# Dividing layer 0's attention probabilities on GpSimd or ScalarE in a kernel whose order is planned, with new strand ranks

## The chip, the cores and the metric

The kernel runs on one core of one Trainium2 chip. The metric is device time in microseconds (us) of one execution, lower is better. The engines are named as in the profile: PE is TensorE's matmul (PEld its weight load), DVE is VectorE, ACT is ScalarE, POOL is GpSimd, SP is SyncE, which only issues DMAs here.

## The reference, cut to what matters

Two transformer layers on 16 x 256 = 4096 tokens of width 128, all in float32; every half layer ends in a residual sum and a layer norm.

```python
# layer 0 attention: 16 heads of 64, over 256 tokens of a batch element
h = rmsnorm(x) * norm_scale
q, k, v = h @ wq, h @ wk, h @ wv               # (16, 256, 16, 64) each
weights = softmax(q * 64**-0.5 @ k^T)          # over 256 keys: the probabilities
x = layernorm(x + (weights @ v) @ w_out + b_out)
# layer 0 feed-forward: 8 routed experts (hidden 256), top 2, and a shared one
x = layernorm(x + shared(x) + sum over top 2 of prob * expert(x))
# layer 1 attention: for each token, 16 heads of 8 attend to each other
scores = q @ k^T / 8                           # (16 x 16) for each token
x = layernorm(x + (softmax(scores) @ v) @ Wproj + bproj)
# layer 1 feed-forward: 8 experts (hidden 512), top 2
x = layernorm(x + sum over top 2 of prob * expert(x))
```

Softmax is exp(s - max) divided by its sum. The change is about who does that division in layer 0's attention, and about the order of everything.

## The kernel before, in words

**Groups, units, parts.** The 4096 tokens are 8 groups of 512 (two batch elements each), held on the chip as tiles `x0` to `x7`. Layer 0's attention works in 128 units: a unit is one pair of heads of one batch element, so a group has 16 units. A unit takes these steps: four score matmuls into a PSUM tile `s` of 128 x 1024 (`scores`, L574); the negated row maximum on DVE (L537); four exponentials on ACT that write `pr` and add up their sums `su` (L543); the reciprocal `rs` on DVE (L554); four multiplications of `pr` by `rs` on POOL (L558, the division); eight transposes of `pr` on PE (`turn`, L591), copied out of PSUM as `pT` (`copied`, L270 on DVE or L272 on ACT); four matmuls with the values into `po` (`attended`, L612), copied out as `oT`. Around these stand the projections `pq`, `pk` (L510) and `pv` (L528) and, once for every half of a group, the output projection `py` (L629, L649). `attention0` walks through the units in order; the transposes and value matmuls of a unit come three units after its scores (`LAG = 3`).

**Waves.** A group whose attention is done goes on as a "part". Parts are joined into waves (`WAVES`): five for layer 0's feed-forward (groups 0, 1, 2+3, 4+5, and 6 with half of 7) and three for layer 1's (0 to 3, 4+5, 6+7). I write (0,4) for layer 0's last wave and (1,2) for layer 1's last. A wave is routed (`chosen`, `route`; L853 writes where each row goes), its rows are scattered to DRAM by expert with indirect DMAs that POOL issues (`send`, L905), read back in blocks of four tiles of 128 rows (`lists`: rows L1014, transposes `px` L1060, first matmuls `ph` L1098, GELU on ACT L1071 or L1077, second matmuls `po_e` L1118, copies `yq`), and gathered again by POOL's indirect DMAs (L934) and added with their gates (L948). Between the layers each part runs through layer 1's attention (`attention1`, `chunk1`), in chunks of 128 tokens. It has no matmuls for scores: products `qk_prod` on DVE (L1216) and their sums (L1220), the maximum, a subtraction on POOL or DVE (L1245), the exponential on ACT (L1254), products `av_prod` with the values in two halves, each on POOL or on DVE (L1292), and sums again on DVE (L1267). After `attention0` is over, a piece of these sums may be done by PE instead (L1226), when the planner finds PE free enough (`SUMS`). The second half of group 7 does not go through the lists: `sequence` and `dense` run all experts over its 256 tokens (`ph_d` L1528, `po_d` L1541).

**The planner.** No scheduler reorders anything. All of the above are Python generators ("strands"). Each yields the time from which its next piece can run and the engine it needs; `everything` (L322) takes again and again the strand with the least start minus `time`, ties by `rank`, and lets it issue one piece. `time` and `rank` are the numbers in `KEYS`; `PACE` gives the rank of the attention units by half group. `work` (L228) advances a clock for each engine by a cost written in the source, for example 2.05 for the four divisions. The order of issue, and so each engine's in-order queue, is fixed when the program is built. The same clocks decide choices between engines: `copied` (L262) takes DVE if its end plus `COPY` is not later than ACT's; `chunk1` takes POOL or DVE for the subtraction and `av_prod` with `FAVOUR` as the margin. `function` (L253) books a change of ACT's function table when exp follows gelu or the other way round; `SWITCH` and `SWITCH_BACK` add to the start of a strand that would need one.

**What the change touches.** `KEYS`, `PACE`, `COPY`, `SUMS`, `FAVOUR`, `SWITCH`, `SWITCH_BACK` (L150 to L194), and `softmax` (L532 to L559), which `scores` starts once for each unit. After the division the unit's time is noted under `end["p", u]`, which `turn` waits for.

Of the kernel before, what the change touches and what calls it, by code (L numbers as in the profile page):

```python
# [10 lines left out]
AF = mybir.ActivationFunctionType  # L11
ALU = mybir.AluOpType
# [25 lines left out]
def two_layers(  # L38
# [23 lines left out]
    nc = tc.nc  # L62
# [75 lines left out]
    def cleared(layer, w):  # L138
# [10 lines left out]

    INF = float("inf")  # L150
    KEYS = {
        "copy qk": (-0.897, 0.036),
        "copy v": (-2, 0.466),
        "copy p": (0.219, 0.818),
        "copy o": (-2, 0.246),
        "softmax": (-0.178, 0.347),
        "softmax 2": (-1.887, 0.235),
        "summed": (-1.203, 0.424),
        "normalised": (-0.822, 0.486),
        "heads": (-0.667, 0.044),  # L160
        "w route": (0.515, 0.015),
        "w send": (0.14, 0.346),
        "w shared": (-0.361, 0.219),
        "w loads": (-0.176, 0.409),
        "w turns 0": (-1.078, 0.086),
        "w turns 1": (1.714, 0.284),
        "w firsts 0": (-1.18, 0.141),
        "w firsts 1": (-0.671, 0.597),
        "w gelu": (-0.639, 0.186),
        "w seconds 0": (-0.71, 0.566),  # L170
        "w seconds 1": (-0.947, -0.095),
        "w stored": (-0.148, -0.464),
        "w gathered 0": (0.897, 0.302),
        "w gathered 1": (1.266, -0.485),
        "w qkv": (2, 0.577),
        "w attention1": (0.922, 0.081),
        "w attention1 2": (0.862, 0.231),
        "w sums": (0.434, 0.099),
        "w normed": (-1.109, 0.178),
        "d loads": (0.367, 1.088),  # L180
        "d route": (-0.611, 0.589),
        "d firsts": (-0.264, -0.008),
        "d gelu": (0.669, 0.244),
        "d seconds": (0.433, -0.444),
        "d added": (0.222, 0.651),
        "d normed": (-0.464, 0.567),
    }
    PACE = [0.305, 1.929, -0.337, -0.416, 1.268, -0.017, 0.106, 1.867]
    PACE += [1.673, 1.567, 1.23, 2, 1.49, 1.385, 1.46, 2]
    now = [0]  # L190
    COPY = -0.089
    SUMS = 9.857
    FAVOUR = 0.474
    SWITCH, SWITCH_BACK = 0.249, 0.734  # L194
    window, unit = [0, 0.0, 1.0], [P]
    clk = {"PE": 0.0, "DVE": 0.0, "ACT": 0.0, "POOL": 0.0, "SP": 0.0}
    table = ["exp"]
    ends = {"t": [0.0] * 2, "m": [0.0] * 2, "s": [0.0] * 2}
    end = {}
# [8 lines left out]
    def paced(at, us, mode):  # L208

        if mode != unit[0]:  # L210
            unit[0] = mode
            us += 0.09
        w = int(at / W)
        if w > window[0]:
            window[2] = 2.0 if w > window[0] + 1 or window[1] < 0.6 * W else 1.0
            window[:2] = w, 0.0
        us *= window[2]
        while at + us > (w + 1) * W:
            part = (w + 1) * W - at
# [42 lines left out]
    def copied(o, i, *after):  # L262
# [50 lines left out]
    def stage(what, w=0, i=0):  # L313

        running[-1].key = key(what, w, i)
# [119 lines left out]
    sc, nm, pr, su, pT, ya = {}, {}, {}, {}, {}, {}  # L435
# [31 lines left out]
    def normalised(g):  # L467
# [10 lines left out]
        yield at, EITHER  # L478
        if max(clk["DVE"], at) + 1.2 + COPY <= max(clk["ACT"], at) + 1.4:
            for c in range(NC):  # L480
# [16 lines left out]
        hT[g] = sb.tile([P, GT], FP, tag="hT", name=f"hT{g}")  # L497
        if max(clk["DVE"], at) + 0.75 + COPY <= max(clk["ACT"], at) + 0.7:
            nc.vector.tensor_scalar(hT[g], t, nscale_s, None, ALU.mult)
# [32 lines left out]
    def softmax(u, place, at):  # L532

        yield at, "DVE"
        nm[u] = sm.tile([P, 4], FP, tag="nm", name=f"nm{u}", bufs=4)
        s = sc[u].rearrange("p j q k -> p (j q) k")
        nc.vector.tensor_reduce(nm[u], s, AX.X, ALU.max, negate=True)  # L537
        at = work("DVE", 1.25, at)
        yield at, "ACT", "exp"
        pr[u] = sb.tile([P, 4, 256], FP, tag="pr", name=f"pr{u}", bufs=LAG + 2)  # L540
        su[u] = sm.tile([P, 4], FP, tag="su", name=f"su{u}", bufs=4)
        for i in range(4):
            nc.scalar.activation(  # L543
                pr[u][:, i, :],
                s[:, i, :],
                AF.Exp,
                bias=nm[u][:, i : i + 1],
                accum_out=su[u][:, i : i + 1],
            )
        at = closed(place, function(2.0, "exp", at))  # L550
        stage("softmax 2")
        yield at, "DVE"
        rs = sm.tile([P, 4], FP, tag="rs", name=f"rs{u}", bufs=4)
        nc.vector.reciprocal(rs, su[u])  # L554
        at = work("DVE", 0.2, at)
        yield at, "POOL"
        for i in range(4):
            nc.gpsimd.tensor_scalar(pr[u][:, i, :], pr[u][:, i, :], rs[:, i : i + 1], 1.0, ALU.mult, ALU.mult)  # L558
        end["p", u] = work("POOL", 2.05, at, one=0.5)  # L559

    def scores(u):

        g, p, b = UNITS[u]
        if g == LAST:
            yield after(("qk", p, b)), "PE", "s"
            q, k = qT[g, p, b], kT[g, p, b]
        else:
            yield after(("q", g, p), ("k", g, p)), "PE", "s"
            q, k = qT[g, p][:, ts(b, 256)], kT[g, p][:, ts(b, 256)]
        sc[u] = ps_s.tile([P, 2, 2, 256], FP, tag="s", name=f"s{u}")  # L570
        for qc in range(2):
            for j in range(2):
                part = slice(j * DH, (j + 1) * DH)
                nc.tensor.matmul(  # L574
                    sc[u][:, j, qc, :],
                    q[part, ts(qc, P)],
                    k[part, :],
                    start=True,
                    stop=True,
                )  # L580
        begin(softmax(u, opened("s"), work("PE", 0.87, mode=-DH)), key("softmax"))
# [84 lines left out]
    def attention0():  # L666
# [3 lines left out]
        for u in range(len(UNITS) + LAG):  # L670
# [4 lines left out]
            if g < NG:  # L675
                now[0] = 2 * g + i // NP
                running[-1].key = (KEYS["heads"][1], PACE[now[0]], 0, 0)
                if i == 3 and g + 1 < NG:
# [522 lines left out]
    def chunk1(w, c, o, qv, kv, at, sums):  # L1201
# [276 lines left out]
    w = DENSE  # L1478
# [185 lines left out]
```

## Time and profile before

| | us |
|---|---|
| runs: lowest, median, highest of three | 1256.01, 1259.93, 1268.71 |
| the profiled execution, its own time | 1225.47 |
| its span from first to last instruction | 1223.8 |
| PE, DVE, ACT, POOL busy in it | 1094.7, 912.3, 730.8, 700.2 |
| last matmul group of layer 0's attention (`py` L649) ends | 852.0 |
| last routing of layer 1, wave (1,2), done (L853) | 1120.8 |

The mean granted TensorE clock of the profiled execution was 0.962 of full speed. Its time is 2.7% under the median of the runs; the page and the trace describe this one execution.

How to read the views quoted below. A row of the page's groups has line, engine, operation, output and input tiles, their shapes and a count, then the total busy time and the mean of one in ns, then the idle time of the engine just before these instructions and what ended it. A row of the windows view is a stretch of time, its length, the busy time of PE, PEld, DVE, ACT and POOL in it with the number of instructions in brackets, the granted clock, the share of DMA time and GB/s. A row of the timeline has start, duration, engine, line and operation. In a waits row one engine's instruction waits for another's; total, number and the longest follow.

### The profile page before, as it was taken

How to read it: one execution, taken by the hardware profiler on the slowest of the kernel's cores; microseconds unless marked ns; L12 is line 12 of the kernel's file. 1: busy time of each engine (PE TensorE's matmuls, PEld its weight loads, DVE VectorE, ACT ScalarE, POOL GpSimd, SP SyncE). 2: the span in 40 equal slices, each digit the busy share in tenths (PEclk: the TensorE clock that was granted, in tenths of full speed). 3: DMA queues.
4: the chain of work that ended last, by engine and by line, in shares of the span. 5: the costliest groups of instructions: out<-in, count | busy, mean ns of one | idle time of the engine just before them, and what ended most of it. 6: DMA issues, size and time to landing. Idle time of an engine off the chain costs nothing.

```text
span 1223.8 us, 22539 instructions
## 1 busy us (share of the span) xinstructions
PE 1094.7 (89%) x7272; PEld 792.6 (65%) x7272; DVE 912.3 (75%) x1810; ACT 730.8 (60%) x2073; POOL 700.2 (57%) x1085
## 2 busy tenths in 40 slices
PE   9999999989999999988999998898667889778893
PEld 5566667666656665576655666675466779678792
DVE  4767786449889789964788888978896879897333
ACT  6556566666667656766566666765554555355442
POOL 4434363635565547732864775577684745567765
PEclk9999999999999999999999999999777999899997
DMA  8900021441000003043100033315627967876871
GB/s 263 276 1 1 1 85 55 143 134 42 3 1 1 2 1 93 29 126 92 29 1 2 16 106 104 94 46 165 192 87 234 280 204 226 258 217 186 250 227 58
DMA packets 187207, 132.45 MB, mean 108 GB/s; under 512 B 12745, under 2 KB 171474, under 8 KB 187090
## 3 DMA queue, kind: packets, MB, share of 16 engines
q1 hardware_dynamic: 179410, 115.27, 32.1%
q0 software_dynamic: 7680, 15.74, 4.2%
q8 instruction: 58, 0.95, 0.3%
q14 instruction: 59, 0.48, 0.1%
HBM read 97.94 MB, written 33.03 MB: 107 GB/s over the span
## 4 chain that ended last, share of the span: by engine, by line
PE 61%; DVE 13%; POOL 11%; ACT 7%; issue 4%; DMA 3%; SPq 1%; ACTq 0%; DVEq 0%; POOLq 0%
PE s L574 10%; PE po L612 9%; PE t L591 8%; POOL rows L905 7%; PE po_e L1118 4%; PE ph L1098 4%; PE pv L528 4%; PE py L629 4%; PE pq L510 4%; PE pk L510 3%; POOL pr L558 2%; DVE av_prod L1292 2%; DVE o L1267 2%; DVE qk_prod L1216 1%; ACT h L1077 1%
## 5 line engine op out<-in xcount | busy, mean ns | idle before, releaser
L558 POOL TENSOR_SCALAR pr<-pr,rs 128x256 f32<-128x256 f32 x512 | 245.8, 497 | 259.6 <-DVE rs L554 172.1
L543 ACT ACTIVATE pr<-s,nm 128x256 f32<-128x256 f32 x512 | 236.0, 476 | 12.3 <-DVE nm L537 9.6
L537 DVE TENSOR_REDUCE nm<-s 128x4 f32<-128x1024 f32 x128 | 156.2, 1220 | 60.2 <-PE s L574 59.6
L1098 PE MATMUL ph<-xqT,wa 128*128 128x128 f32 x1028 | 141.0, 293 | 26.1 <-ACT h L1077 9.0
L905 POOL DMA_INDIRECT rows<-x,r_pi x120 | 131.9, 1099 | 40.9 <-issue 20.6
L1098 PEld LDWEIGHTS ph<-xqT,wa 128*128 128x128 f32 x1028 | 131.9, 204 | 35.1 <-ACT h L1077 11.6
L934 POOL DMA_INDIRECT y<-outs,r_pi x120 | 122.5, 1021 | 52.9 <-issue 23.1
L591 PE MATMUL t<-ident,pr 128*128 128x128 f32 x1024 | 141.8, 279 | 4.9 <-ACT pT L272 1.7
L612 PE MATMUL po<-pT,v 128*64 128x256 f32 x1024 | 141.0, 394 | 2.2 <-DVE kT L270 0.9
L591 PEld LDWEIGHTS t<-ident,pr 128*128 128x128 f32 x1024 | 111.5, 141 | 48.4 <-POOL pr L558 23.0
L270 DVE COPY pT<-t 128x512 f32<-128x512 f32 x171 | 111.7, 686 | 35.4 <-PE t L591 35.0
L574 PEld LDWEIGHTS s<-kT,qT 64*128 64x128 f32 x896 | 77.5, 187 | 82.4 <-issue 65.8
L574 PE MATMUL s<-kT,qT 64*128 64x256 f32 x896 | 127.9, 404 | 0.0
L272 ACT COPY oT<-po 128x256 f32<-128x256 f32 x102 | 38.0, 373 | 137.1 <-PE po L612 136.9
L543 ACT ACTIVATION_READ_ACCUMULATOR pr<-s,nm 128x1 f32 x512 | 105.9, 207 | 0.0
L612 PEld LDWEIGHTS po<-pT,v 128*64 128x64 f32 x1024 | 63.0, 136 | 62.2 <-issue 18.3
L1292 POOL TENSOR_TENSOR av_prod<-sc,qkv 128x1024 f32<-128x1024 f32 x34 | 86.4, 2550 | 28.7 <-ACT sc L1254 28.3
L1216 DVE TENSOR_TENSOR qk_prod<-qkv 128x1024 f32<-128x1024 f32 x64 | 82.9, 1295 | 0.0
L1267 DVE TENSOR_REDUCE o<-av_prod 128x64 f32<-128x1024 f32 x64 | 75.8, 1200 | 8.5 <-POOL av_prod L1292 8.2
L1220 DVE TENSOR_REDUCE sc<-qk_prod 128x128 f32<-128x1024 f32 x64 | 78.1, 1220 | 2.2
L1118 PE MATMUL po_e<-wb,h 128*128 128x128 f32 x648 | 76.3, 276 | 2.1 <-DVE lg L738 1.5
L1118 PEld LDWEIGHTS po_e<-wb,h 128*128 128x128 f32 x648 | 74.4, 192 | 3.6 <-DVE lg L738 1.9
(230 smaller groups left out, 1972.6 us busy)
## 6 DMA issues: line engine op xcount, KB each, us to landing
wa<-in_w_dram SPq DMA_DIRECT2D x190, 128.0 KB
wa<-in_w_dram SPq DMA_DIRECT2D x81, 256.0 KB
wb<-in_w_dram SPq DMA_DIRECT2D x81, 256.0 KB
xq<-rows SPq DMA_DIRECT2D x38, 256.0 KB
outs<-yq SPq DMA_DIRECT2D x38, 256.0 KB
rows<-clear SPq DMA_DIRECT2D x3, 1472.0 KB
rows<-clear SPq DMA_DIRECT2D x1, 2496.0 KB
rows<-clear SPq DMA_DIRECT2D x2, 1216.0 KB
```

What stands on the lines that cost most here:

```text
L270: nc.vector.tensor_copy(o, i)
L537: nc.vector.tensor_reduce(nm[u], s, AX.X, ALU.max, negate=True)
L543: nc.scalar.activation(pr[u][:, i, :], s[:, i, :], AF.Exp, bias=nm[u][:, i : i + 1], accum_out=su[u][:, i : i + 1],)
L558: nc.gpsimd.tensor_scalar(pr[u][:, i, :], pr[u][:, i, :], rs[:, i : i + 1], 1.0, ALU.mult, ALU.mult)
L574: nc.tensor.matmul(sc[u][:, j, qc, :], q[part, ts(qc, P)], k[part, :], start=True, stop=True,)
L591: nc.tensor.transpose(t[:, kc, ts(qc, P)], pr[u][:, 2 * j + qc, ts(kc, P)], ident)
L612: nc.tensor.matmul(po[j * DH : (j + 1) * DH, :], vs[g, p // 4, 2 * b + kc][:, ts(h, DH)], pT[u][j][:, kc, :], start=(kc == 0), stop=(kc == 1),
L905: i = nc.gpsimd.indirect_dma_start(out=rows[layer][w][:, :], out_offset=bass.IndirectOffsetOnAxis(ap=r.pos[:, k, c : c + 1], axis=0), in_= ...
L934: nc.gpsimd.indirect_dma_start(out=y, out_offset=None, in_=outs[layer][w][:, :], in_offset=bass.IndirectOffsetOnAxis(ap=r.pos[:, k, c0 + c ...
L1098: nc.tensor.matmul(ph[:, q - q0, c, :], was[i, q][0][:, c, :], xTs[i][0][:, q, :], start=True, stop=True)
L1118: nc.tensor.matmul(po[:, q, :], hs[i, q][0][:, c, :], wbs[i, q][0][:, c, :], start=(c == 0), stop=(c == nh - 1))
L1292: (nc.gpsimd if e == "POOL" else nc.vector).tensor_tensor(m, sc1[:, ts(j, HALF)].unsqueeze(2).to_broadcast(full), v3.unsqueeze(1).to_broad ...
```

## The change

The division of a unit's probabilities (L558) may now be issued on ACT too: as four activations with the identity function and the reciprocal as scale. The planner takes POOL if the end it sees there is not later than ACT's end plus `FAVOUR`. All ranks and times of the strands, the paces and the margins have new values; `FAVOUR` goes from 0.474 to 1.062, `SUMS` from 9.857 to 4.434. No other function differs. Lines of the changed kernel from L557 on are shifted: the division on POOL is L559 there, on ACT L563, and everything behind it stands five lines lower.

```diff
     KEYS = {
-        "copy qk": (-0.897, 0.036),
-        "copy v": (-2, 0.466),
-        "copy p": (0.219, 0.818),
+        "copy qk": (0.304, 0.033),
+        "copy v": (-0.269, 0.523),
+        "copy p": (0.383, 1.08),
...
-        "softmax": (-0.178, 0.347),
-        "softmax 2": (-1.887, 0.235),
+        "softmax": (-0.066, 0.509),
+        "softmax 2": (-1.427, 0.071),
...
     }
-    PACE = [0.305, 1.929, -0.337, -0.416, 1.268, -0.017, 0.106, 1.867]
-    PACE += [1.673, 1.567, 1.23, 2, 1.49, 1.385, 1.46, 2]
+    PACE = [1.852, -1.516, -1.265, -1.123, 0.732, 0.983, 1.152, 1.417]
+    PACE += [0.679, 0.685, 1.48, 0.579, 0.99, -1.924, -0.939, 1.947]
     now = [0]
-    COPY = -0.089
-    SUMS = 9.857
-    FAVOUR = 0.474
-    SWITCH, SWITCH_BACK = 0.249, 0.734
+    COPY = 0.039
+    SUMS = 4.434
+    FAVOUR = 1.062
+    SWITCH, SWITCH_BACK = 0.202, 0.754
...
         at = work("DVE", 0.2, at)
-        yield at, "POOL"
-        for i in range(4):
-            nc.gpsimd.tensor_scalar(pr[u][:, i, :], pr[u][:, i, :], rs[:, i : i + 1], 1.0, ALU.mult, ALU.mult)
-        end["p", u] = work("POOL", 2.05, at, one=0.5)
+        yield at, ("POOL", "ACT")
+        if max(clk["POOL"], at) + 2.05 <= max(clk["ACT"], at) + 1.55 + FAVOUR:
+            for i in range(4):
+                nc.gpsimd.tensor_scalar(pr[u][:, i, :], pr[u][:, i, :], rs[:, i : i + 1], 1.0, ALU.mult, ALU.mult)
+            end["p", u] = work("POOL", 2.05, at, one=0.5)
+        else:
+            for i in range(4):
+                nc.scalar.activation(pr[u][:, i, :], pr[u][:, i, :], AF.Identity, scale=rs[:, i : i + 1])
+            end["p", u] = work("ACT", 1.8, at)
```

More of the change, by code (lines that the diff above doesn't have):

```diff
@@ L151, in two_layers @@
     KEYS = {
-        "copy qk": (-0.897, 0.036),
-        "copy v": (-2, 0.466),
-        "copy p": (0.219, 0.818),
-        "copy o": (-2, 0.246),
-        "softmax": (-0.178, 0.347),
-        "softmax 2": (-1.887, 0.235),
[L158 to L186, printed above, removed]
-    }
-    PACE = [0.305, 1.929, -0.337, -0.416, 1.268, -0.017, 0.106, 1.867]
-    PACE += [1.673, 1.567, 1.23, 2, 1.49, 1.385, 1.46, 2]
+        "copy qk": (0.304, 0.033),
+        "copy v": (-0.269, 0.523),
@@ new lines, in two_layers @@
+        "copy p": (0.383, 1.08),
+        "copy o": (-1.601, 0.246),
+        "softmax": (-0.066, 0.509),
+        "softmax 2": (-1.427, 0.071),
+        "summed": (-0.419, 0.032),
+        "normalised": (1.073, 0.277),
+        "heads": (-0.14, 0.067),
+        "w route": (0.494, 0.045),
+        "w send": (0.024, 0.635),
+        "w shared": (0.015, 0.221),
+        "w loads": (0.751, 0.707),
+        "w turns 0": (-2, 0.087),
+        "w turns 1": (0.32, 0.252),
+        "w firsts 0": (-1.424, 0.003),
@@ new lines, in two_layers @@
+        "w firsts 1": (0.944, 0.425),
+        "w gelu": (-0.985, 0.05),
+        "w seconds 0": (-0.027, 0.661),
+        "w seconds 1": (0.954, -0.017),
+        "w stored": (-0.96, -0.326),
+        "w gathered 0": (-1.281, 0.211),
+        "w gathered 1": (0.908, -0.251),
+        "w qkv": (-1.924, -0.099),
+        "w attention1": (0.606, 0.031),
+        "w attention1 2": (1.33, 0.612),
+        "w sums": (1.189, 0.386),
+        "w normed": (0.453, 0.071),
+        "d loads": (-1.231, 1.034),
@@ L190, in two_layers @@
+        "d route": (0.724, 0.275),
+        "d firsts": (-0.348, 0.727),
+        "d gelu": (-0.236, -0.148),
+        "d seconds": (-0.088, -0.189),
+        "d added": (0.797, 0.1),
+        "d normed": (-0.245, 0.781),
+    }
+    PACE = [1.852, -1.516, -1.265, -1.123, 0.732, 0.983, 1.152, 1.417]
+    PACE += [0.679, 0.685, 1.48, 0.579, 0.99, -1.924, -0.939, 1.947]
     now = [0]
-    COPY = -0.089
-    SUMS = 9.857
-    FAVOUR = 0.474
-    SWITCH, SWITCH_BACK = 0.249, 0.734
+    COPY = 0.039
```

## The prediction

> **What bounds the kernel now.** I read the page's busy lines and its 40 slices first.
>
> ```profile
> span 1223.8 us, 22539 instructions
> ...
> PE 1094.7 (89%) x7272; PEld 792.6 (65%) x7272; DVE 912.3 (75%) x1810; ACT 730.8 (60%) x2073; POOL 700.2 (57%) x1085
> ...
> PE   9999999989999999988999998898667889778893
> ...
> DVE  4767786449889789964788888978896879897333
> ...
> PEclk9999999999999999999999999999777999899997
> ```
>
> For 28 slices (856 us) PE is full at full clock: layer 0's attention. Then PE drops to 6 to 8 tenths, and DVE stands at 8 or 9. POOL and ACT, between which the change shifts the division, bound neither part. The timeline of PE gives the pace of the first part:
>
> ```profile
> 121.31 1.13 PE L574 MATMUL s<-kT,qT 64*128 64x256 f32 x8
> 122.37 1.08 PE L612 MATMUL po<-pT,v 128*64 128x256 f32 x8
> 123.39 1.09 PE L591 MATMUL t<-ident,pr 128*128 128x128 f32 x8
> 124.32 1.02 PE L510 MATMUL pq<-hT,wq 128*128 128x512 f32 x2
> 125.27 1.13 PE L574 MATMUL s<-kT,qT 64*128 64x256 f32 x8
> ```
>
> From start to start: scores 1.06 us, values 1.02, transposes 0.93, a projection 0.95; a unit takes 3.96 us with nothing between. With such distances for every PE instruction (the lists' matmuls 0.118 each: 32 of `po_e` took 3.84) I sum PE's work ahead of each unit. Ahead of unit 32 the sum is 161.1 us, and the trace starts it at 164.7: apart from the start, PE lost nothing. Up to the last `py` the sum is 789 (and 4 us of start) and the trace has 852: 59 us lost, 51 of them in three stretches, where feed-forward pieces come between the units. The windows view has these (units 32 to 48, 72 to 88, 112 to the end of attention) and then the part behind attention in three pieces:
>
> ```profile
> 164.70:303.60 138.90, 130.21 (x866) 90.67 (x866) 89.53 (x189) 94.89 (x273) 71.22 (x123) 1.00 0.34 100
> 435.80:571.70 135.90, 124.99 (x814) 86.29 (x813) 102.15 (x182) 88.35 (x256) 68.76 (x111) 0.99 0.25 74
> 698.90:852.00 153.10, 141.36 (x950) 103.27 (x949) 129.07 (x255) 101.89 (x291) 102.67 (x143) 0.98 0.33 97
> 852.00:1108.00 256.00, 198.00 (x1393) 177.21 (x1392) 218.42 (x392) 135.58 (x251) 157.07 (x192) 0.89 0.72 212
> 1108.00:1148.00 40.00, 32.74 (x241) 30.37 (x241) 19.77 (x91) 18.47 (x36) 29.23 (x46) 1.00 0.76 229
> 1148.00:1224.00 76.00, 53.36 (x427) 51.71 (x427) 27.10 (x111) 27.39 (x54) 45.59 (x59) 0.86 0.51 151
> ```
>
> PE's work in the first three is 126.6, 118.6 and 131.9 us: 12.3, 17.3 and 21.2 lost. From 852 to 1108 DVE is busy 218 of 256 us: it bounds (layer 1's attention). From 1108 to 1148 the last wave is routed and scattered; from 1148 its lists run on PE to 1192, and 32 us of gathering, norm and store follow.
>
> The rows that the change touches, from the groups and the waits:
>
> ```profile
> L558 POOL TENSOR_SCALAR pr<-pr,rs 128x256 f32<-128x256 f32 x512 | 245.8, 497 | 259.6 <-DVE rs L554 172.1 <-PE pv L528 40.2 <-PE t L591 14.9
> L543 ACT ACTIVATE pr<-s,nm 128x256 f32<-128x256 f32 x512 | 236.0, 476 | 12.3 <-DVE nm L537 9.6 <-DVE rs L554 0.9 <-POOL pr L558 0.7
> L1292 POOL TENSOR_TENSOR av_prod<-sc,qkv 128x1024 f32<-128x1024 f32 x34 | 86.4, 2550 | 28.7 <-ACT sc L1254 28.3 <-DVE o L1267 0.3
> L1292 DVE TENSOR_TENSOR av_prod<-sc,qkv 128x1024 f32<-128x1024 f32 x30 | 53.7, 1789 | 4.6 <-ACT sc L1254 4.5
> L1254 ACT ACT_TABLE_LOAD x19 | 24.4, 1283 | 0.3
> ```
>
> ```profile
> PE t L591 <- POOL pr L558: 0.4, 1, 0.4
> ```
>
> The last line is all that PE's matmuls waited for a division: it is hidden behind three units (`LAG`), and POOL waits for `rs` 172 us in all. So the new branch by itself can win 0.4 us; what counts is what the new order does.
>
> **The change part by part.** Counts are from the orders of the two built programs.
>
> *The division.* 14 of 128 units go to ACT (none before unit 16, three between units 72 and 80, three after 112). POOL loses 14 x 1.92 = 27 us (245.8 / 128 each). On ACT the form is new; between the copy of `po` of the same shape (373 ns) and the exponential (476), four take 1.5 to 1.9 us; nearer the latter, as it reads a scale: 1.7, 24 us in all. Identity activations (L409, L485) show no table load in the trace. Behind it on ACT queue copies of `po` and `t` and the next exponentials; ACT is at 60%, PE has two banks of each kind, and I cost this at nothing. Without that cover it is 24 us.
>
> *Function tables.* ACT's table loads go from 64 to 52, 33 to 27 before attention ends. In the first stretch 12 loads become 8 with the same PE work (126.6); its loss is 12.3 us, 1.03 for each load, so 4 loads are worth 4. In the second, 11 become 8 (PE 117.9), and the feed-forward block that stood within units 84 to 88 (ACT 53 of PE's 56 us of work, 11 loads) is spread over 76 to 84 (ACT 60 of 74, 7 loads): 17.3 / 11 x 3 = 5. Bounds: nothing (the loads lay beside a wait for PE itself), to 7 x 1.28 = 9 and half of the remaining loss, 18.
>
> *The third stretch.* Here units 116 to 120 have 54 us of DVE work beside 44 of PE, and took 56: DVE bound them. The larger of the two, in steps of four units, sums to 146.5 before and 136.3 after (worst: the last four, 40.7). That is 10; but there are 10 table loads for 8: I take 7, ends 0 and 12.
>
> So attention ends 16 us earlier, at 836 (ends 0 and 30). 4 us of PE work that stood before its end now stand behind it; they are in the counts below.
>
> *Behind attention, to the routing of (1,2).* DVE's work is 249 us before (the trace took 269, with 13 for the last chain of small instructions), 231 after: 7 `av_prod` fewer on DVE (12.5 us), 4 subtractions fewer (2), copies that go to ACT (4), two sums that become 16 matmuls (1), against one more routing. At the trace's rate (255 us for 243 of work) 18 fewer are 19.
>
> Here the Trainium skill speaks against the change: "SBUF — State Buffer", section "Who interferes with whom", says that a DVE instruction with two SBUF inputs and a GpSimd one that reads SBUF exclude each other, whichever comes later waiting for the whole of the other. The row agrees that it happens: `av_prod` on DVE takes 1.21 us where POOL is idle and up to 3.27 where POOL works on the other half, mean 1.79; and one `qk_prod` took 4.15 for 1.21. There will be 47 `av_prod` on POOL for 34, 6 of the 13 behind attention. By the row alone each of them frees 1.79 us of DVE; by the rule each can hold a `qk_prod` back by half of 2.55. For 6 that would be 8 us of the 19. But the waits in the row (30 x 0.58 = 17 us) are mostly those of DVE's half for POOL's half of one chunk, which vanish when both are on POOL; all `qk_prod` together lost 64 x 0.08 = 5. I take 3.
>
> POOL's work up to here rises from 157 to 175 us of some 250: no bound. So (1,2) is routed 253 us after attention instead of 269.
>
> *The rest.* From routing to the last `po_e` took 71 us: 27 for sends (16 at 1.1) and rows, with 22 of PE work beside them, and 44 of lists. After: 29 us of PE work beside the sends, and 8 gathers more on POOL among them (8 x 1.02): 32; lists 43: 75. Then 32 us of gathering as before. The dense strand, of which 21 us instead of 9 of PE work now stand behind the last `po_e`, needs some 21 + 8 for additions, norm and store, and fits beside it.
>
> Behind attention: 253 + 75 + 32 = 360 for 372, 12 less; I count 11, for the dense strand's fit is close. In all 16 + 11 = 27 of the span's 1224: 1197. The median of the runs is 1259.93, 2.95% above this span; the trace doesn't show why, and I carry the ratio: 1197 x 1.0295 = 1232.
>
> **Rivals.**
> 1. *Hidden anyway, no change.* The loads in the first two stretches lay beside PE's own latency, and the last routing comes no earlier, since DVE's 38 idle us in 852 to 1108 are waits for PE and POOL that stay. For it: PE waited on `o` and `x` there, and POOL's chains of `n_r`, `n_nb` stand before ACT's norms. Against: DVE at 85%. What is left is the third stretch and a little: 8 us, 1216, so 1252.
> 2. *ScalarE in the way: slower.* A division of 1.7 us on ACT stands ahead of a copy of `po` (0.37) and of `t` (0.59); if PE is out of banks then, each costs up to 2.7, 14 of them 38. Against the 27 of gain that is 11 more: 1235, so 1271. It decides from 27 / 14 = 1.9 us exposed per division. For it: ACT's work is four fifths of PE's in the first two stretches. Against: the planner takes ACT only where it is free earlier by its clocks, and the three units of lag.
> 3. *More.* The second stretch keeps only the loss of its loads not shared with PE, and DVE's savings move everything behind attention without the port's 3 and with the clock higher (0.89 in 852 to 1108): 45 us, 1179, so 1214.
> 4. *The branch does nothing, the ranks and `FAVOUR` all.* A time of 1232 too; it differs only in what undoing the branch alone would show.
>
> **How the numbers follow.** Forecast (with 4): 0.50, own range 1218 to 1246. Rival 1: 0.22. Rival 2: 0.15. Rival 3: 0.13. About 1% is what a measurement of this kernel can tell from no change: under 1247.3 is faster, over 1272.5 slower. Rival 2 straddles that border in its spread; I leave it at slower, as other misfits of the order can add to it. Faster 0.63, same 0.22, slower 0.15. The range runs from between 3 and its better end to rival 2: 1206 to 1270.
>
> **What would show it.** Right: unit 48 starts 4 us earlier than at 303.6, unit 88 9 us earlier than at 571.7, attention ends near 836; 52 table loads; `av_prod` on DVE near 1.5 us mean and DVE busy under 90% in the 250 us behind attention; the last routing some 253 us after it. Wrong: losses at units 72 to 80 or behind 112 with PE waiting for ACT behind the new divisions; `qk_prod` with a mean over 1.5; the end set by `po_d`, not by the gathers of (1,2). A different ratio of runs to profiled execution would break the last step alone.

## The result, and the profile after

The changed kernel takes 1315.48 us (median of 4 runs, 1311.81 to 1316.87), the kernel before beside it 1262.39: a ratio of 1.0425, interval 1.0377 to 1.0474. It is slower; 1232 was forecast. The runs for the record and the experiments were made on several chips: the kernel before takes 1262 us in the runs for the record, 1226 to 1228 on three chips (called A, B and D here) and 1278 on a fourth (C), and the first trace of before (span 1223.8) looks like those of A, B and D. Which chip the runs for the record had is not known; I call it the chip of the record. B, C and D were each used at one time only, so what I put down to a chip may also be its state at that time.

The page of the changed kernel on the chip of the record, its busy lines and 40 slices:

```profile
span 1314.2 us, 22521 instructions
...
PE 1144.5 (87%) x7304; PEld 821.7 (63%) x7304; DVE 879.7 (67%) x1784; ACT 741.3 (56%) x2120; POOL 694.5 (53%) x1042
...
PE   9999998899999869999999999785856986885785
...
PEclk9999999799999878999999999896777998997898
```

DVE has 33 us less to do than before, yet the clock line now has holes within the attention (the 8th and the 14th to 16th slice), where it had none. The windows view, with the stages of the prediction (units 32 to 48, 72 to 88, 112 to the end of attention, then to the routing of (1,2), on to 1206 while its rows are sent and read, and to the end; columns: us, busy PE, PEld, DVE, ACT, POOL with counts, clock, DMA share, GB/s):

```profile
164.60:314.00 149.40, 137.87 (x865) 95.21 (x864) 90.64 (x195) 95.59 (x282) 79.31 (x122) 0.93 0.32 94
450.70:597.90 147.20, 132.09 (x808) 89.03 (x807) 65.48 (x152) 87.66 (x257) 57.49 (x99) 0.92 0.26 76
726.90:885.90 159.00, 142.24 (x934) 102.82 (x933) 121.26 (x238) 94.47 (x266) 87.99 (x119) 0.97 0.32 93
885.90:1172.00 286.10, 215.18 (x1404) 187.92 (x1405) 220.59 (x420) 130.57 (x255) 167.40 (x210) 0.85 0.62 183
1172.00:1206.00 34.00, 21.93 (x148) 20.30 (x147) 9.37 (x25) 9.30 (x17) 20.62 (x32) 0.75 0.45 138
1206.00:1314.00 108.00, 78.44 (x563) 72.22 (x562) 37.52 (x161) 40.70 (x79) 58.67 (x75) 0.91 0.58 169
```

Attention ends at 885.9, not at 836, and the part behind it takes 428 us for 372. Every stage of the attention is longer than before (149.4 for 138.9 us, 147.2 for 135.9, 159.0 for 153.1), with nearly the same number of PE instructions. The same program on chip B (run e9), the same stages (the fifth ends at 1140):

```profile
164.90:302.10 137.20, 129.33 (x865) 90.53 (x864) 91.18 (x196) 95.69 (x282) 79.62 (x122) 1.00 0.35 103
438.70:567.80 129.10, 124.05 (x808) 84.65 (x808) 66.17 (x152) 87.27 (x257) 57.35 (x99) 0.98 0.29 87
696.60:850.70 154.10, 141.24 (x934) 103.40 (x933) 122.62 (x238) 94.08 (x266) 87.89 (x119) 0.97 0.32 96
850.70:1108.30 257.60, 204.04 (x1401) 178.29 (x1401) 223.65 (x419) 130.96 (x255) 171.07 (x209) 0.89 0.67 203
1108.30:1140.00 31.70, 26.43 (x204) 24.77 (x203) 14.93 (x48) 15.41 (x27) 26.04 (x39) 0.95 0.77 237
1140.00:1224.00 84.00, 65.34 (x510) 61.72 (x508) 32.36 (x139) 34.87 (x70) 53.42 (x68) 0.95 0.64 185
```

There attention ends at 850.7 and all takes 1224.0. So there are two questions: why the 27 us of gain did not come at all (e9), and what adds 90 us on the chip of the record. The groups that the change touches, on the chip of the record (busy us, mean ns | idle before), and below them one of the kernel before:

```profile
L559 POOL TENSOR_SCALAR pr<-pr,rs 128x256 f32<-128x256 f32 x456 | 222.4, 506 | 318.8 <-DVE rs L554 207.7 <-PE pv L528 47.2 <-PE t L596 19.5
L563 ACT ACTIVATE pr<-pr,rs 128x256 f32<-128x256 f32 x56 | 23.9, 504 | 13.9 <-issue 8.6 <-DVE rs L554 5.3
L1297 POOL TENSOR_TENSOR av_prod<-sc,qkv 128x1024 f32<-128x1024 f32 x47 | 115.8, 2475 | 37.1 <-ACT sc L1259 24.3 <-DVE o L1272 5.7 <-DVE sc L1225 5.2
L1297 DVE TENSOR_TENSOR av_prod<-sc,qkv 128x1024 f32<-128x1024 f32 x17 | 25.3, 1504 | 1.2 <-ACT sc L1259 0.9
L1221 DVE TENSOR_TENSOR qk_prod<-qkv 128x1024 f32<-128x1024 f32 x64 | 92.5, 1447 | 19.4 <-ACT qkv L272 19.3
```

```profile
L1216 DVE TENSOR_TENSOR qk_prod<-qkv 128x1024 f32<-128x1024 f32 x64 | 82.9, 1295 | 0.0
```

A division on ACT takes 0.504 us; four overlap a little and take 1.71 us from the first start to the last end, as the 1.7 taken. `av_prod` on DVE has the mean of 1.50 that was named. `qk_prod` has grown from 1.295 to 1.447.

### The profile page after: what moved, and what is told of

Same layout as the page of the kernel before. It is cut to its first block, busy times and chain, and to the rows that moved or that the text cites. A ratio compares the mean times of both kernels' runs of the same rounds, so it can differ in the third digit from the quotient of the medians.

```text
span 1314.2 us, 22521 instructions
## 1 busy us (share of the span) xinstructions
PE 1144.5 (87%) x7304; PEld 821.7 (63%) x7304; DVE 879.7 (67%) x1784; ACT 741.3 (56%) x2120; POOL 694.5 (53%) x1042
## 4 chain that ended last, share of the span: by engine, by line
PE 64%; DVE 13%; ACT 8%; issue 6%; POOL 5%; another core or an unknown queue 4%; DMA 1%; ACTq 0%; POOLq 0%; DVEq 0%
PE s L579 9%; PE po L617 9%; PE t L596 8%; PE ph L1103 6%; PE po_e L1123 6%; PE pv L528 4%; PE pq L510 3%; PE py L634 3%; PE pk L510 3%; DVE qk_prod L1221 2%; DVE sc L1225 2%; PE po L1191 2%; ACT h L1082 1%; POOL y L939 1%
## 5 line engine op out<-in xcount | busy, mean ns | idle before, releaser
L559 POOL TENSOR_SCALAR pr<-pr,rs 128x256 f32<-128x256 f32 x456 | 222.4, 506 | 318.8 <-DVE rs L554 207.7
L1103 PE MATMUL ph<-xqT,wa 128*128 128x128 f32 x1028 | 150.1, 299 | 60.6 <-ACT h L1082 18.4
L1103 PEld LDWEIGHTS ph<-xqT,wa 128*128 128x128 f32 x1028 | 136.1, 208 | 74.1 <-ACT h L1082 20.9
L617 PE MATMUL po<-pT,v 128*64 128x256 f32 x1024 | 148.0, 401 | 10.7 <-DVE pT L270 7.8
L910 POOL DMA_INDIRECT rows<-x,r_pi x120 | 122.9, 1024 | 51.4 <-DVE r_pi L858 26.9
L1297 POOL TENSOR_TENSOR av_prod<-sc,qkv 128x1024 f32<-128x1024 f32 x47 | 115.8, 2475 | 37.1 <-ACT sc L1259 24.3
L270 DVE COPY pT<-t 128x512 f32<-128x512 f32 x166 | 108.2, 685 | 34.9 <-PE t L596 28.6
L1221 DVE TENSOR_TENSOR qk_prod<-qkv 128x1024 f32<-128x1024 f32 x64 | 92.5, 1447 | 19.4 <-ACT qkv L272 19.3
L1123 PE MATMUL po_e<-wb,h 128*128 128x128 f32 x648 | 79.8, 282 | 5.6 <-ACT h L1076 4.4
L1076 ACT ACTIVATE h<-ph 128x512 f32<-128x512 f32 x81 | 47.1, 595 | 63.4 <-PE ph L1103 43.5
```

The lines of the kernel that those rows point to most:

```text
L617: nc.tensor.matmul(po[j * DH : (j + 1) * DH, :], vs[g, p // 4, 2 * b + kc][:, ts(h, DH)], pT[u][j][:, kc, :], start=(kc == 0), stop=(kc == 1),
L910: i = nc.gpsimd.indirect_dma_start(out=rows[layer][w][:, :], out_offset=bass.IndirectOffsetOnAxis(ap=r.pos[:, k, c : c + 1], axis=0), in_= ...
L1103: nc.tensor.matmul(ph[:, q - q0, c, :], was[i, q][0][:, c, :], xTs[i][0][:, q, :], start=True, stop=True)
L1123: nc.tensor.matmul(po[:, q, :], hs[i, q][0][:, c, :], wbs[i, q][0][:, c, :], start=(c == 0), stop=(c == nh - 1))
L1221: nc.vector.tensor_tensor(m, q3[:, ts(j, HALF)].unsqueeze(2).to_broadcast(full), k3.unsqueeze(1).to_broadcast(full), ALU.mult)
L1297: (nc.gpsimd if e == "POOL" else nc.vector).tensor_tensor(m, sc1[:, ts(j, HALF)].unsqueeze(2).to_broadcast(full), v3.unsqueeze(1).to_broad ...
```

## The experiments

**Is it the place, the order, or the engine of the division?** Five runs on chip A. The first is the kernel before again.

> The kernel before, unchanged, to have a second trace of it. Its profiled execution had 1224 us of span where its runs have a median of 1262. If the 37 us are a chance of that execution, this trace has a span near 1255, more half-clock time than the 94 us of the first one, and perhaps stretches in which SP's register instructions take 0.7 us instead of 0.05, of which the first trace had none and the changed kernel's has some 31. If it repeats, the span is near 1225 and the half-clock time near 94 us.

1226.25 us, ratio 0.9994 (0.9978 to 1.001): the time of the first trace comes again, not the 1262 of the record.

The changed order, its 14 divisions issued on POOL in their places:

```diff
-                nc.scalar.activation(pr[u][:, i, :], pr[u][:, i, :], AF.Identity, scale=rs[:, i : i + 1])
+                nc.gpsimd.tensor_scalar(pr[u][:, i, :], pr[u][:, i, :], rs[:, i : i + 1], 1.0, ALU.mult, ALU.mult)
```

> The changed kernel's planned order, every instruction in its place, but the 14 divisions that it gives to ScalarE are issued on GpSimd at the same place. Theory A (the new order itself costs the time, who divides hardly matters): 1305 to 1325 us, as the changed kernel's 1315. Theory B (a division on ScalarE holds back the copies and exponentials queued behind it): the 14 divisions' 24 us or more come back: under 1292. Theory C (the divisions that left GpSimd let its indirect DMAs run back to back, 16 in 19 us at unit 72 to 76, and the other engines' dispatch stalls beside them): the burst is cut up by three divisions, the stall of unit 72 to 76 (some 15 us) goes away: 1295 to 1305.

1241.51, ratio 1.0122 (1.0086 to 1.0158).

The order of before, the same 14 units divided on ACT in their places:

```diff
+            if u in (19, 33, 53, 63, 70, 72, 73, 74, 86, 88, 101, 111, 124, 125):
+                nc.scalar.activation(pr[u][:, i, :], pr[u][:, i, :], AF.Identity, scale=rs[:, i : i + 1])
```

> The kernel before in its own order, but the divisions of the 14 units that the changed kernel gives to ScalarE (19, 33, 53, 63, 70, 72, 73, 74, 86, 88, 101, 111, 124, 125) are issued on ScalarE in place. Theory A: within 1% of the kernel before. Theory B: 24 to 38 us slower, 1286 to 1300. Theory C: small, since few of these units lie beside bursts of indirect DMAs in this order: within 1%.

1229.89, ratio 1.0021 (1.0009 to 1.0033).

The new ranks without the branch, planned afresh (the diff of the change, its branch taken out):

```diff
-        yield at, ("POOL", "ACT")
-        if max(clk["POOL"], at) + 2.05 <= max(clk["ACT"], at) + 1.55 + FAVOUR:
+        yield at, "POOL"
```

> All new ranks, paces and margins, but the division only on GpSimd, planned anew. Theory A: 1300 to 1330, the ranks alone carry the loss. Theory B and C: 1260 to 1285, the branch carries it. As the planner's order shifts with every choice, 10 us either way say nothing.

1314.75, ratio 1.0715 (1.0681 to 1.075).

The changed kernel itself:

> The changed kernel once more, beside the kernel before on this chip, and beside e2. In e2 (same order, divisions on GpSimd) SP's register instructions never took 0.7 us, in the changed kernel's first trace they did, in five stretches. If that dispatch stall belongs to the place (the chip, where the kernel before took 1262 too, not 1227), this run gives 1.01 to 1.02 times the kernel before (1240 to 1252) where the kernel before takes 1227, without long register instructions. If it belongs to the divisions on ScalarE, it is there again: 1.04 times and more, 1275 to 1315.

1232.94, ratio 1.0043 (1.0024 to 1.0062), where the record has 1.0425. ScalarE is not in the way: in the changed order the divisions on it save 8.6 us (e2 to e5), in the order of before they cost 0.2%. And the ranks do not carry the change alone, as rival 4 had it: planned without the branch they lose 7%.

**The branch with the old ranks**, planned afresh: 76 of 128 units then go to ACT.

> The kernel before with the new branch alone, ranks and margins as before, planned anew. With the old FAVOUR of 0.474 the planner puts the division on ScalarE for 76 of 128 units, and the order around it shifts. If a division on ScalarE is hidden: within 2% of the kernel before. If it stands in the way of copies and exponentials (0.5 us or more exposed each, as PE is the bound): 38 us slower or more, 1265 and up. If GpSimd's freed time is worth something: faster than 1215.

1307.3, ratio 1.0639 (1.0597 to 1.0681). Later, on chip B, that order with all 128 divisions issued on POOL (the edit of e2):

> The order that the ranks of before give with the branch (76 of 128 units planned on ScalarE), but all 128 divisions issued on GpSimd in their places. It separates the engine of the division from the order. Theory A (the order is what loses 6.4%: ScalarE only did what it was planned to do): 1330 or more, since GpSimd now carries 76 x 2.05 = 156 us more in an order that did not plan for it. Rival B (76 divisions on ScalarE hold the scores back and are the loss themselves): back towards the kernel before, 1230 to 1280.

1328.34, ratio 1.0849 (1.0803 to 1.0895). So ScalarE as engine gains some 21 us there too (across two chips); the order loses. In e4, e6 and e10 TensorE is at half clock for 183 to 201 us, 97 in before (e1): a change of the ranks or of the candidates alone redraws the whole order, and these redrawn orders cost 6 to 8%. Which misfits they have was not examined.

**The price of a table load.** GELU is left out (an identity in its place), so ACT switches tables once; first in the order of before, then in the changed one.

```diff
-                nc.scalar.activation(h[:, 0], ph[:, 0], AF.Gelu)
+                nc.scalar.activation(h[:, 0], ph[:, 0], AF.Identity)
```

> The kernel before in its own order with the identity function where GELU stood (so the experts are linear: GELU is left out). ScalarE's table loads go from 64 to 1; everything else stays. The prediction's price of 1.03 to 1.57 us of PE time for each load in the mixed stretches: attention would end 33 to 43 us earlier, near 815 instead of 852, and the kernel at 1180 or less. If the loads lie beside waits that stay: attention ends within 10 us of 852, the kernel at 1205 to 1227.

1212.6, ratio 0.9886 (0.9855 to 0.9917). Attention ends at 840 instead of 852: its 33 loads are worth 12 us, 0.37 each, where one lasts 1.283.

> The same (identity for GELU, so no GELU) in the changed kernel's order: 52 loads become 1. If loads explain the mixed stretches' loss in both orders, this ends up as fast as e7 or faster (fewer DVE instructions), within 10 us. If the new order loses time by its own cross-engine waits, it stays 10 to 25 us above e7.

1222.75, ratio 0.9963 (0.9947 to 0.9978). The changed order stays 10 us behind also without loads, so they are not what separates the two.

**Work behind the sends.** Both orders put long runs of sends on POOL behind the attention (24 or more, most 1.27 us apart), with other POOL work queued among and behind them. The timeline of e9 (changed kernel, chip B), rows of the shared expert's weights:

```profile
925.55 0.18 DVE L1492 TENSOR_TENSOR r_wd<-r_scratch 128x16 f32<-128x16 f32 x1
...
934.43 0.12 POOL L1495 MEMSET r_wd<- 128x2 f32 x1
...
934.61 0.59 PE L1499 MATMUL pw<-ident,r_wd 128*9 128x128 f32 x2 [12.09 <-POOL apart L909]
```

The weights are there at 925.7; the column of ones beside them stands behind the sends until 934.5, and TensorE waits 12.1 us, ready matmuls behind it. With these ones on DVE, in each kernel (the same edit is made where the other waves write such ones, five more memsets):

```diff
-            nc.gpsimd.memset(r.w[:, :, NE:NE0], 1.0)
+            nc.vector.memset(r.w[:, :, NE:NE0], 1.0)
```

> The changed kernel once more. Theory A (the 4% of record belongs to the place in which it was measured: there the sequencers stall beside GpSimd's indirect sends; the program itself costs +0.4%): if the kernel before takes 1227 us here, this takes 1229 to 1237 with no SyncE register instruction over 0.2 us; if the kernel before takes about 1262 here, this takes about 1315 and the trace has the long register instructions again. Rival B (the program has two outcomes of its own, whatever the place): 1315 can come beside a kernel before of 1227, or 1233 beside one of 1262.

> The kernel before with the ones beside the weights of the shared expert written by VectorE instead of GpSimd, six instructions in all. In the trace of before the transposition of those weights waits 10.1 us at 882.7 (its weights are there at 890.8, the ones at 892.7 because they stand behind 20 us of sends on GpSimd), with ready matmuls of TensorE behind it. Theory A (that idle stretch and the half clock after it, 20.4 + 10.2 us at half speed nearby, are on the path): the stretch shrinks from 10.1 to about 8 us there, and by what the other five sites give: -2 to -6 us, 1221 to 1225. Rival B (the weights themselves come as late): no change, 1227.

> The changed kernel with the same six instructions on VectorE. Here the weights are there at 931.2 and the ones only at 940.0, so TensorE idles 12.1 us from 928.0, 8.8 of them for the ones, with the shared expert's second half ready behind it. Theory A (the sends on GpSimd, moved by the new order in front of the ones, cost the changed kernel what its other savings brought): 8.8 us and some half clock less, 1220 to 1226, below both the changed kernel (1233) and the kernel before (1227). Rival B (what stands behind it waits for the sends themselves): no change, 1231 to 1235.

On chip B the changed kernel took 1231.25 (1.0035, 1.0018 to 1.0051), before with ones on DVE 1227.06 (1.0012, 1.0 to 1.0024), the changed kernel with them 1226.13 (0.9993, 0.9973 to 1.0013). So these memsets are all of the changed kernel's +0.35%, and they cost the kernel before nothing. In e12 the wait at `pw` is 3.27 us:

```profile
929.02 0.18 DVE L1492 TENSOR_TENSOR r_wd<-r_scratch 128x16 f32<-128x16 f32 x1
929.14 0.06 DVE L1495 MEMSET r_wd<- 128x2 f32 x1
...
929.26 0.46 PE L1499 MATMUL pw<-ident,r_wd 128*9 128x128 f32 x2 [3.27 <-DVE r_wd L1495]
```

But 6 of these 9 us come back as a longer wait for `x` (3.89 us in e9), behind products of weights and values that also stand behind the sends:

```profile
953.86 1.65 PE L1340 MATMUL pqkv<-wqkv,xT 128*128 128x384 f32 x2 [9.70 <-DVE x L1566]
```

Before has the same: its ones alone gave nothing, the wait for `o` after it only grew (8.22 us in e16, 13.94 in e11). So ones and products together went to DVE, two products in before, three and a subtraction in the changed kernel (counted in POOL's order):

```diff
-            (nc.gpsimd if e == "POOL" else nc.vector).tensor_tensor(
+            sidestep("av", e, (21, 22)).tensor_tensor(
```

These came to chip C, with the changed kernel beside them:

> The changed kernel once more, on whichever chip it comes to. Theory A (the 4% of record belong to the chip that it was measured on): beside a kernel before of 1227 it takes 1229 to 1237 and no SyncE register instruction lasts over 0.2 us; beside a kernel before of about 1262 it takes about 1315, and some 30 register instructions last 0.7 us. Rival B (the program has two outcomes of its own): 1315 beside a kernel before of 1227, or 1233 beside one of 1262.

> The changed kernel with the ones of the shared expert on VectorE as before, and with three products of weights and values (945 to 952 in the run with the ones moved) and one subtraction of maxima (933.6) taken from behind the 24 sends on GpSimd and given to VectorE. There VectorE's sum waits 4.5 us for the first of them, its next product takes 4.36 instead of 1.16 us beside them, and TensorE's wait for x lasts 9.70 us from 944.2. Theory A (the work behind the sends is what the changed kernel loses there): VectorE takes 3 x 1.16 + 0.4 us more, the wait shrinks by 5 to 9 us and the time to 1217 to 1223, below the kernel before. Rival B (VectorE is itself the bound behind the attention, 245.6 us of its 348): no gain, 1224 to 1230.

> The same for the kernel before: ones on VectorE, and the two products that stand behind its 32 sends (927.8 and 930.1, where VectorE's sum waits 10.1 us and TensorE 13.9 us from 918.7) on VectorE. Theory A (work behind the sends sets this stretch): 8 to 12 us less of that wait, 1214 to 1220. Rival B (the stretch is made good by slack behind it, as with the ones alone, which changed nothing): 1225 to 1229.

There before takes 1278.33, the changed kernel 1321.12 (1.0366, 1.0306 to 1.0425), its cleared form 1334.27 (1.0435, 1.0395 to 1.0475), and the cleared form of before 1264.59 (0.9902, 0.9878 to 0.9927). On chip D, the last three:

> The kernel before once more, for a trace of it beside the next run on the same chip. On a chip where it takes about 1227 us: no SyncE register instruction over 0.2 us, half-clock time near 97 us. On a chip where it takes 1260 to 1280: theory A (stalls beside GpSimd's sends, of which the changed kernel's denser bursts make more) expects about half as many long register instructions as the 29 and 31 of the changed kernel, 12 to 20; rival B (the changed kernel stalls no more than this one and loses by its order alone) expects as many, 25 to 35.

> The changed kernel with eight small memsets instead of one between two of the 60 + 60 sends of rows on GpSimd, some 0.8 us more from send to send (1.27 to about 2.1). On a chip without stalls it costs what it lengthens: theory 0, 120 x 0.8 = 96 us of GpSimd time, of which the tail's bursts stand on the path, 20 to 50 us. On a chip with stalls: theory A (another engine's sequencer waits only while a send is being issued, so that what counts is the share of time in which sends stand back to back) expects the stalls gone or halved, fewer than 15 long register instructions, and a loss against the changed kernel smaller than on the other chips or a gain; rival B (each send has a fixed price for the others) expects 25 to 35 of them and 20 to 50 us more.

```diff
-                nc.gpsimd.memset(apart, 0.0)
+                for _ in range(8):
+                    nc.gpsimd.memset(apart, 0.0)
```

> The kernel before with the ones and the two products from behind the sends on VectorE, again, on whichever chip it comes to. Theory A (work queued behind the sends is a cost of the order itself): 0.7 to 1.2% less than the kernel before on a chip of either kind, 1214 to 1219 beside 1227. Rival B (the gain of 1.0% needs the stalls of the chip where it was seen): within 0.3% of the kernel before beside 1227.

Before again 1228.24 (1.0, 0.9988 to 1.0013); the changed kernel with thinned sends 1341.95 (1.0934, 1.0901 to 1.0967), far past the 20 to 50 us expected. Sends that follow each other are 2.31 us apart there, not 2.1, and PE falls behind e9 by 12 us at 190, 14 at 470 and 27 at 930 (e9's time), all behind a routing; at `pw` alone TensorE waits 38 us. The cleared form of before took 1218.77, ratio 0.9932 (0.9907 to 0.9958): it beats both kernels on C, and before on D. What it removes there, by PE's timeline of before (e16) and of the cleared form (e18):

```profile
921.22 0.49 PE L419 MATMUL t_x<-ident,o 128*128 128x128 f32 x3
929.93 0.48 PE L419 MATMUL t_x<-ident,o 128*128 128x128 f32 x1 [8.22 <-DVE o L1308]
```

```profile
921.58 0.49 PE L419 MATMUL t_x<-ident,o 128*128 128x128 f32 x3
924.79 0.47 PE L419 MATMUL t_x<-ident,o 128*128 128x128 f32 x1 [2.73 <-DVE o L1316]
```

**What chip C does.** In no run did the changed kernel take some 1315 us beside a kernel before of 1227, or 1233 beside one of 1262 or more: the slow times belong to where, or when, the program runs. PE's timeline at the same place of the same program, on chip B (e9) and then on C (e13); 15 sends run on POOL from 444.8 to 463.7 on B, from 455.5 to 474.4 on C:

```profile
453.51 1.09 PE L596 MATMUL t<-ident,pr 128*128 128x128 f32 x8
454.44 1.02 PE L510 MATMUL pk<-hT,wk 128*128 128x512 f32 x2
455.30 1.02 PE L528 MATMUL pv<-wv,hT 128*128 128x512 f32 x2
456.25 1.14 PE L579 MATMUL s<-kT,qT 64*128 64x256 f32 x8
457.31 1.08 PE L617 MATMUL po<-pT,v 128*64 128x256 f32 x8
```

```profile
461.63 1.14 PE L579 MATMUL s<-kT,qT 64*128 64x256 f32 x8
467.90 1.09 PE L617 MATMUL po<-pT,v 128*64 128x256 f32 x2 [5.13 <-DVE pT L270]
473.50 1.97 PE L617 MATMUL po<-pT,v 128*64 128x256 f32 x6 [4.52 <-DVE pT L270]
```

The copies that PE waits for are late themselves, and so is everything else. On the chip of the record the same place shows it as idle time of DVE and ACT that no instruction of the profile explains (`issue`: the engine waited for nothing that is seen; `remote`: for something that is not of this core or not known):

```profile
471.78 0.69 DVE L270 COPY qT<-pq 128x512 f32<-128x512 f32 x1 [2.84 <-issue]
...
472.59 1.70 ACT L563 ACTIVATE pr<-pr,rs 128x256 f32<-128x256 f32 x4 [8.60 <-issue]
...
478.15 1.23 DVE L537 TENSOR_REDUCE nm<-s 128x4 f32<-128x1024 f32 x1 [5.60 <-remote]
```

Even SP's register steps between two weight loads, 0.03 to 0.05 us in every trace of A, B and D, take up to 0.7: over 0.35 us are 29 of them in e13, 31 on the record, 18 in e14 and 16 in e15, none elsewhere. POOL's sends keep their pace (0.96 us each), and the DMA packets' mean times do not differ (0.035 us in the hardware queue in all traces). I take runs of at least 8 sends with less than 0.6 us between two, and in each four sends of a run add the busy shares of PE, DVE and ACT (durations summed, at most 1 for each engine, so 3 is full). Means over the runs that are so long, some of them over two or three runs or one:

```
sends                     1-4    5-8    9-12   13-16  17-20  21-24  25-27
e9      changed, B        2.19   2.23   2.09   2.29   0.50
e16     before, D         1.88   2.19   1.93   2.16   3.00   2.32   0.05
e13     changed, C        2.08   1.76   1.18   1.24   0.80
record  changed           2.20   1.64   1.23   1.02   0.81
e14     changed, clear, C 2.25   1.51   0.80   1.11   1.00   0.01   0.00
e15     before, clear, C  1.98   1.97   2.81   2.34   2.10   1.34   1.00
```

On B and D the engines work on through a run, until they wait for POOL itself (the 0.50 and the 0.05 are single runs in which PE waits for the ones and for the products). On C and on the chip of the record the changed order fades from the fifth send or so. The order of before, in its cleared form, does so less: its run of 27 (e15) fades from the 21st. So the length of a run alone does not decide. In e14 the edit had removed POOL's own work from among the sends: 27 follow each other, until 971.7, and from 963.2 to 974.5 all three engines stand still, though every matmul ahead of ACT's next `h` had ended by 955.6:

```profile
974.52 1.14 ACT L1082 ACTIVATE h<-ph,r_bias 128x128 f32<-128x128 f32 x4 [22.79 <-remote]
975.71 2.07 PE L1103 MATMUL ph<-xqT,wa 128*128 128x128 f32 x8 [20.15 <-ACT h L1082]
```

Compared instruction by instruction, PE falls 38 us behind e13 between 920 and 940 (e13's time), and ends 22 us behind: there clearing made the changed kernel worse.

## Why the prediction was wrong, point by point

**The last step, 1197 x 1.0295, took the slower runs for a scale that holds for any order.** Compared instruction by instruction with e9, the record's PE falls behind by 11 us at 220 to 240 (e9's time), 16 at 450, 22 at 900 (9 of them come back), 9 at 1050, 13 at 1110 and 6 at 1140, all at runs of sends; at the end it is 90 us behind. So does that of e13: TensorE's gaps grow from 102 to 162 us, its half-clock time from 93 to 173. The changed order has 12 runs of 8 or more sends in e9 (144 of the 240), before has 5 in e16 (69): there, divisions of the attention on POOL, 1.85 us for a unit, stand between the sends (around 470 to 490, for instance), where the new order has 15 back to back. Most of this comes with the order: with all its divisions on POOL it still has 10 runs (121 sends, e2), and the old order with 14 units on ACT keeps its 5 (e3). At the record before loses 35 us against chips A, B and D, the changed kernel 83; on C they lose 51 and 89. The ratio carried 35 over, so this step misses 48 of the error of 83.

What stays open: that the runs of sends cause the stalls is argued from where the time is lost, not shown. Fewer sends in a row were not tried on a chip that stalls (e17, with its thinned sends, ran on D), before has no uncleared trace on one, and why these chips stall is not known. One lead: in the changed order transfers of instructions come at 9 in 100 us on the average, behind the fifth send of a run at 8 on A and B (10 in 122 us each) but at 2 or 3 on the record and C (2 in 103 us, 3 in 105). At the place above they come at 455.8 and 456.2 on B, within the run, and at 478.1 and 479.8 on C, after it. Whether engines stand because instructions come late or the reverse, the traces don't tell.

**The gain itself did not come** (the other 35 us: 1232 on chips A and B against 1197, 3 of them between trace and runs; that 1232 is also the forecast for the slower runs is chance):
- *Division at nothing:* right, and a little better. ACT's form took the 1.7 us of the estimate, and nothing on PE waits for it.
- *Function tables:* wrong in price. A load is worth 0.37 us (e7), not 1.03 to 1.57. The first stretch lost 10.6 us for 12.3, but without loads the fall is as large (9.8 in e7 to 8.2 in e8). The second lost 11.1 for 17.3, so the 5 us came; without loads it falls from 13.1 (e7) to 11.1 (e8), so about 4 of the 6 can be the loads', and 2 are not.
- *Third stretch:* wrong. Up to unit 127 it loses 20.5 us, before 17 to 20; the seven us from the sum of the larger of DVE and PE are not there. DVE's work does not set what the feed-forward block between the units takes, as the prediction read it. In before, units 116 to 120 took 55.7 us with DVE busy for 47.9, and in e9 the block stands in units 120 to 124 and took 54.1 with DVE busy for only 39.6, PE's work being about the same. What holds it instead is not shown. Units 48 to 72 and 88 to 112, not examined, lose 6 us more (8.3 for 4.5, 6.4 for 4.1). Attention ends at 850.7 and 856.5, with before at 849.2 and 852.0: no gain for 16.
- *Behind attention:* the routing of (1,2) ended 259.6 us after attention in e9, 268.9 in before: 9 of the 16 came, and not by less work. From the end of attention to that routing DVE is busy for 245 us in e9 (240 in e5) and 243 in before (e16); the 18 fewer are not there. Six `av_prod` fewer on DVE, not seven, gave 9.7 us, but others took longer. DVE's instructions beside an `av_prod` of POOL outlasted their usual time by 27.4 us (17 of them) in e9 and 23 in e5 and on the record, against 14 (11 of them) in before: 8 to 13 more, where 3 were taken. (As usual I take the 15th percentile of the same instruction's times in the trace, and count what exceeds it by over 0.3 us.) So the port's share was mis-sized. The rule of the Trainium skill ("SBUF — State Buffer", "Who interferes with whom") spoke against the change, and the 8 us that the prediction estimated by it, for `qk_prod` alone, were nearer. The growth of `qk_prod` on the record, 64 x (1.447 - 1.295) = 9.7 us, single ones lasting 3.4 beside POOL's `av_prod`, lies for more than half within the attention. It hangs on what meets what, not on the number moved: in e7, where no `av_prod` was moved, the mean is 1.451 too.
- *The rest:* the last step of lists gave it back. From routing to the last `po_e` 83 us, not 75 (before 72.6), and 30.6 to the end. The tail takes 373 for 372. The ones behind the sends, a wait of TensorE that no step of the sum had, cost 5 us in the medians (e9 to e12).

On chips A and B the outcome is that of rival 1, no change, or a shade slower; on the record it is a slower case that no rival had. Rival 2, ScalarE in the way, is refuted by e2 and e3.

## What to carry to other kernels

When an order changes, look at what comes to stand closer together in each queue: here the new order, more than the divisions taken off GpSimd, joined its indirect sends into runs, and things queued behind a run (a memset of 0.12 us, two products) made TensorE wait 8 to 12 us. Try such producers on an engine whose queue is short: the ones and two products together took 0.7 to 1.0% off the kernel before, the ones alone nothing, and on the chip that stalls the same edit made the changed kernel 1% slower. A wait that is removed can come back at the next one. And where trace and runs differ by 3%, do not carry the ratio over to a new order before knowing where the difference arises.

## What was not expected of the hardware

The same program took 1231 to 1233 us on two chips, 1321 on a third and 1315 in the runs for the record; the kernel before took 1226 to 1228 on three chips, 1278 and 1262 there. In the changed kernel the difference sits beside runs of GpSimd's indirect DMAs, where the other engines slow from the fifth send or so and can stop (0.00 of 3 engines busy in e14), and in TensorE's half-clock time (93 us in e9, 173 in e13); whether the runs are its cause is not shown. A table load of 1.283 us was worth only 0.37.
